# A two-layer graph kernel: the gather table split at row block 10, pauses of three one-column writes, stores by four blocks, the dense branch's flag computed early

## The chip, the core and the metric

The kernel runs on one core of a Trainium2 chip. The metric is device time in microseconds from the first to the last instruction. Before the change it is 416.93 us, the median of three runs (416.52 to 417.89). The profile that is read below is of one further execution, whose instructions span 423.4 us; times of day within it are counted from its first instruction.

## The reference

Two layers over N = 2708 nodes with D = 128 features and an adjacency matrix `adj` that is sparse (each row normalised, a diagonal of self-loops). Layer 0 is hyperbolic: a product of `adj` with node vectors, then functions of norms row by row. Layer 1 passes messages:

```python
XW = mobius_matvec(W, X)
gamma = 2.0 / jnp.maximum(1.0 - jnp.sum(XW * XW, axis=-1, keepdims=True), EPS)
two_mean = (A_hat @ (gamma * XW)) / _clamp_abs(A_hat @ (gamma - 1.0))
...
s = node_feats @ msg_w[:, :D].T
d = node_feats @ msg_w[:, D:].T
messages = jax.nn.gelu(s[:, None, :] + d[None, :, :] + msg_b, approximate=False)
aggregated = jnp.einsum('ijd,ij->id', messages, adj)
combined = jnp.concatenate([node_feats, aggregated], axis=-1)
new_feats = combined @ upd_w.T + upd_b
h = jax.nn.gelu(new_feats, approximate=False) + node_feats
```

Each layer ends with a layer norm of its result plus its input; layer 1 has one more within. A message is needed only where `adj[i, j]` is not zero.

## The kernel before

The nodes are cut into 22 row blocks of 128 (the last has 20 rows). **Layer 0** goes block by block (`layer0`, L327): a load of the block's transposed columns `aT` (L330), its signs (L332), 22 accumulating matmuls with the node vectors (L337), each of two passes. Beside it the kernel finds each block's non-zeros: `keys` (L353) encodes their positions by matmuls of the signs, `extract` (L380) ranks them and lays them into tiles of 128 edges. There are 99 such tiles in all (`TILES`); a tile has a one-hot matrix `R`, and for each of its 128 edges a column index `J` and a flat address `F`.

When a chunk of row blocks is done (`CHUNKS`), `layer0_end` (L471) finishes layer 0 for it, computes `s` and `d` for its rows and stores `d` into `table` in DRAM (L545). It is a generator that is advanced between the halves of the following blocks, by `PARTS`.

**Gathers.** GpSimd reads per tile, with indirect DMAs (`gather`, L195): 128 values of `adj` at the addresses `F` into a column of `V` (L466), and 128 rows of `table` at the indices `J` into `dd` (L675). Behind each gather stands a pause: one addition of two 128x128 tiles into `gap`, which nobody reads (L200). [...]

**Split.** Columns of the first `SPLIT` row blocks are ranked apart from the rest, so that some tiles of each block refer to them alone ("early" tiles; `LATE` counts the others, "late"). A gather of an early tile reads only the first `SPLIT * 128` rows of `table`, so it waits only for the first chunk. Late tiles read the whole table, and wait for all of layer 0.

**Messages.** Tiles are put together by four (a "quad"; `work`, L663): first the early tiles of blocks 0 to 7, then for each block what is left. `fetch` (L670) gathers a quad into one of seven rooms (`RING`). `messages` (L678) handles a quad: matmuls spread `s` to the edges (L687), VectorE makes the weighted one-hot `rv` (L689) and adds the gathered `dd` (L692), ScalarE applies gelu (L693), TensorE sums by row (L702). When a block's last tile is summed, `node` (L619) is queued: the update matmuls into the single bank `sel` (L571 to L574), gelu (L575), layer norms in groups of 8, 6, 4, 2 and 2 blocks (`finish`, L577), and a store of each block (L606). `step` (L633) advances the queue after each quad. An inverse root is computed by 11 VectorE instructions (`rsqrt`, L223), except in the last group, where GpSimd takes a power (`inverse_root`, L561).

**Flag.** The kernel has a dense branch for inputs whose non-zeros don't fit the tiles. From L770 on counts are compared and summed over partitions, and every engine loads the flag (L822) and branches.

A scheduler puts the instructions of each engine into one order, by priority and the order of the code; each engine then runs its own in that order, waiting on semaphores. DMAs that SyncE issues (block loads, table stores, output stores) are in one such order too.

Of the kernel before, what the change touches and what calls it, by code (L numbers as in the profile page):

```python
# [10 lines left out]
F32 = mybir.dt.float32  # L11
# [4 lines left out]
OP = mybir.AluOpType  # L16
AX = mybir.AxisListType

P = 128
# [4 lines left out]
MAGIC = 1597463007.0  # L24
FAR = 6.103033
BREAKS = (11, 18)
CHUNKS = [(0, 13), (13, 18), (18, 22)]
PARTS = (0, 1, 2, 2)
GROUPS = [(0, 8), (8, 6), (14, 4), (18, 2), (20, 2)]
EARLY = 8  # L30
# [2 lines left out]

SPLIT, BITS = 13, 16
RING = 7


def group_of(b):  # L40

    if b == 0:
        return [
            [(0, 1, 8), (1, 2, 8)],
            [(2, 4, 8), (4, 6, 4), (6, 8, 4)],
            [(8, 10, 4), (10, 13, 4), (13, 14, 4), (14, 16, 4)],
            [(16, 19, 4), (19, 22, 4)],
        ]
    if b == 1:
        return [[(0, 4, 4), (4, 8, 2), (8, 13, 2), (13, 22, 2)]]  # L50
    return [[(0, 4, 2 if b < 9 else 1), (4, 13, 1), (13, 22, 1)]]

TILES = [6, 6, 5, 3, 8, 7, 5, 5, 4, 4, 4, 4, 4, 3, 3, 4, 3, 3, 3, 3, 3, 3, 3, 2, 1]
LATE = [0, 0, 2, 3, 3, 3, 2, 2, 2, 2, 2, 2, 2, 1, 1, 2, 1, 1, 2, 2, 2, 2, 2, 1, 1]
SPAN = 8192.0


# [18 lines left out]
def hyperbolic_then_message_kernel(  # L79
# [10 lines left out]
    nc = tc.nc  # L90
# [4 lines left out]
    rows = [min(P, N - b * P) for b in range(NB)]  # L95
# [6 lines left out]
    const = ctx.enter_context(tc.tile_pool(name="const", bufs=1))  # L102
# [7 lines left out]
    w0_sb, wT, rowvec, o = pk[:, :D], pk[:, D : 5 * D].rearrange("p (i d) -> p i d", d=D), {}, 5 * D  # L110
# [13 lines left out]
    ones = const.tile([P, P], F32, name="ones")  # L124
    nc.gpsimd.memset(ones, 1.0)

    nhalf = const.tile([P, 1], F32, name="nhalf")
# [43 lines left out]
    J = const.tile([P, NT], U32, name="J")  # L171
    V = const.tile([P, NT], F32, name="V")
# [17 lines left out]

    of_block = {b: [l for l, v in enumerate(LISTS) if v[0] == b] for b in range(NB)}

    gap = const.tile([P, P], F32, name="gap")

    def gather(o, src, at):  # L195
        last = nc.gpsimd.indirect_dma_start(  # L196
            out=o, out_offset=None, in_=src, in_offset=bass.IndirectOffsetOnAxis(ap=at, axis=0)
        )
        with tc.issue_after(last.ins), tc.high_priority():
            nc.gpsimd.tensor_add(gap, ones, ones)  # L200

    mx = big.tile([P, NB, D], F32, name="mx")
    y = big.tile([P, NB, D + 2], F32, name="y")
# [19 lines left out]
    def rsqrt(v, n, pool=None, two=False):  # L223

        if two:
            h, t, o = (sc.tile([P, 2, NB], F32, name=f"two{k}")[:, :, :n] for k in range(3))
            h = h.bitcast(I32)
        elif pool is None:
            h, t, o = cols(n).bitcast(I32), cols(n), cols(n)
        else:  # L230
            h = pool.tile([P, n], I32, name="rh")
            t = pool.tile([P, n], F32, name="rt")
            o = pool.tile([P, n], F32, name="ro")
        nc.vector.tensor_scalar(h, v.bitcast(I32), 1, None, op0=OP.arith_shift_right)
# [46 lines left out]
    for g, n in quads:  # L281
# [98 lines left out]
    def extract(l):  # L380

        b, groups, c0, wa, wb, t0, n, late = LISTS[l]
# [25 lines left out]
        op = bank("sel", 1)  # L408
# [8 lines left out]
        for k, _ in parts:  # L417
            first = n - late if k and wa else 0
            dl = deg[:, l, k + 1 : k + 2]
            for k0 in range(first, n, 4):  # L420
# [3 lines left out]
                o = flat(R[:, t0 + k0 : t0 + k1, :])  # L424
# [19 lines left out]
        F = small.tile([P, TMAX], U32, name="F", bufs=12)  # L444
        step = 512 // (C + 1)
        for k0 in range(0, n, step):
            k1 = min(n, k0 + step)
            w = k1 - k0
            t = slice(t0 + k0, t0 + k1)
# [13 lines left out]
                F[:, k0:k1], J[:, t], float(b * P * N - 1), rid[:, t], op0=OP.add, op1=OP.add  # L463
            )
        for t in range(t0, t0 + n):
            gather(V[:, t : t + 1], adj.rearrange("i (j o) -> (i j) o", o=1), F[:, t - t0 : t - t0 + 1])  # L466

    x1, x1T, gd = x_sb, xT, nom
    s_nm = mx
# [88 lines left out]
            nc.vector.bn_stats(st[:, k - k0, :], v[:, k, :])  # L558
            nc.vector.bn_aggr(mv[:, k, :], st[:, k - k0, :])

    def inverse_root(ve, n, pool, last):  # L561
        if not last:
            return rsqrt(ve, n, pool)
        o = pool.tile([P, n], F32, name="ro")
        nc.gpsimd.tensor_tensor(o, ve, nhalf[:, 0:1].to_broadcast([P, n]), op=OP.pow)
        return o

    def update(h, k, b, ags):
        up = bank("sel", 1)
        s = slice(b * P, (b + 1) * P)  # L570
# [6 lines left out]
    def finish(h, b0, n, pool, last):  # L577

        mv = mvs.pop(b0)
        ve = pool.tile([P, n], F32, name="ve1")  # L580
        nc.vector.tensor_scalar_add(ve, mv[:, :, 1], LN_EPS)
        rs = inverse_root(ve, n, pool, last)
        yield
        st = pool.tile([P, n, 6], F32, name="st1")
        mw = pool.tile([P, n, 2], F32, name="mv1")
        for k in range(n):
            v = h[:, k, :]
            nc.vector.scalar_tensor_tensor(v, v, mv[:, k, 0:1], rowvec["lw"], op0=OP.subtract, op1=OP.mult)
            nc.vector.scalar_tensor_tensor(v, v, rs[:, k : k + 1], xlb[:, b0 + k, :D], op0=OP.mult, op1=OP.add)
            moments(h, st, mw, [k])  # L590
            if k % 2 and k + 1 < n:
                yield
        ve = pool.tile([P, n], F32, name="ve1")
        nc.vector.tensor_scalar_add(ve, mw[:, :, 1], LN_EPS)
        yield
        rs = inverse_root(ve, n, pool, last)
        if not last:
            nb = pool.tile([P, n], F32, name="nb")
            nc.vector.scalar_tensor_tensor(nb, mw[:, :, 0], -1.0, rs, op0=OP.mult, op1=OP.mult)
        for k in range(n):  # L600
            v, r = h[:, k, :], rows[b0 + k]
            if last:
                nc.vector.tensor_scalar(v, v, mw[:, k, 0:1], rs[:, k : k + 1], op0=OP.subtract, op1=OP.mult)
            else:
                nc.scalar.activation(v, v, AF.Identity, scale=rs[:, k : k + 1], bias=nb[:, k : k + 1])
            nc.sync.dma_start(out[(b0 + k) * P : (b0 + k) * P + r, :], h[:r, k, :])  # L606
        yield

    mvs = {}
# [21 lines left out]
    queue = []  # L631

    def step():  # L633

        for g in list(queue):
            if next(g, queue) is queue:
                queue.remove(g)
# [14 lines left out]
    early, late, soon = {}, {}, set()  # L652
# [10 lines left out]
    work = fours([(b, early[b]) for b in range(EARLY)], True)  # L663
# [3 lines left out]
    done = [0]  # L667
    group = {b: (g0, gn) for g0, gn in GROUPS for b in range(g0, g0 + gn)}

    def fetch():  # L670

        if len(rooms) < (len(work) if whole else ahead):
            dd = edge.tile([P, 4, P], F32, name="dd", bufs=RING)
            for k, (_, t, *_) in enumerate(work[len(rooms)]):
                gather(dd[:, k, :], table[: SPLIT * P] if t in soon else table, J[:, t : t + 1])  # L675
            rooms.append(dd)

    def messages():  # L678

        q, ts = done[0], work[done[0]]  # L680
        done[0] += 1
        w = len(ts)
        dd = rooms[q][:, :w, :]
        X = bank("kx" if q >= ahead and q % 2 else "X").rearrange("p (t d) -> p t d", d=D)[:, :w, :]
        rv = edge.tile([P, 4, P], F32, name="rv", bufs=2)
        for k, (b, t, *_) in enumerate(ts):
            nc.tensor.matmul(X[:, k, :], lhsT=R[:, t, :], rhs=s_nm[:, b, :], start=True, stop=True)  # L687

            nc.vector.tensor_scalar(  # L689
                rv[:, k, :], iotaN, rid[:, t : t + 1], V[:, t : t + 1], op0=OP.is_equal, op1=OP.mult  # L690
            )
        nc.vector.tensor_tensor(dd, X, dd, op=OP.add)  # L692
        nc.scalar.activation(dd, dd, AF.Gelu)  # L693
        for k, (b, t, first, final, before) in enumerate(ts):
            mine = before or b >= EARLY
            if first:
                while len(sums) > 2:
                    step()
                sums[b] = bank("mp", 3)
                if mine:  # L700
                    own(b, sums[b])
            nc.tensor.matmul(  # L702
                sums[b][:, :P], lhsT=dd[:, k, :], rhs=rv[:, k, :], start=(first and not mine), stop=final
            )
            if final and before:
                nc.scalar.copy(gd[:, b, :D], sums.pop(b)[:, :P])  # L706
            elif final:
                g0, gn = group[b]
                queue.append(node(gd[:, g0 : g0 + gn, :D], b - g0, b, g0, gn, [gd[:, b, :D]] if b < EARLY else []))
        fetch()  # L710
        step()

# [48 lines left out]
        fetch()  # L761
    for g, n in quads:
        nc.vector.tensor_add(xlb[:, g : g + n, :D], x1[:, g : g + n, :], wide(rowvec["lb"], n))
    while done[0] < len(work):
        messages()
    while queue:
        step()


    bad = sc.tile([P, NL], F32, name="bad")  # L770
# [18 lines left out]
    for i, v in enumerate(seconds):  # L789
        k = v.shape[1]  # L790
# [27 lines left out]
    nc.vector.tensor_add(tot[:, 0:1], tot[:, 0:1], tot[:, 2:3])  # L818
    flag = sc.tile([P, 1], I32, name="flag")
    nc.vector.tensor_copy(flag, tot[:, 0:1])  # L820

    dense = nc.values_load(flag[0:1, 0:1], min_val=0, max_val=2 * P + 1)  # L822
    with tc.If(dense > 0):
# [100 lines left out]
```

## Time and profile before

| what | value |
|---|---|
| time, median of three | 416.93 us |
| span of the profiled execution | 423.4 us |
| TensorE, VectorE, ScalarE, GpSimd busy | 318.6, 302.9, 200.2, 292.1 us |
| first V gather, first table gather, last gather | 46.7, 199.9, 390.6 us |
| last table store issued | 277.3 us |
| DMA queues' mean rate | 107 GB/s |

The profile has a page and views of the same trace. The page shows the span in 40 slices of 10.6 us, one digit of busy time for each engine. Groups put together the instructions of one line and form: how many, busy time, mean time of one in ns, and the idle time before them with what ended it. A timeline lists instructions in order. A table of stretches gives each engine's busy time within them and the clock that TensorE was granted. [...]

### The profile page before, as it was taken

The page shows a single profiled execution, that of the slowest core. Times are in us where ns is not written, and L with a number is a line of the kernel's source. Part 1 is how long each engine was busy: PE and PEld are TensorE (multiplying, and loading weights), DVE is VectorE, ACT ScalarE, POOL GpSimd, SP SyncE. Part 2 cuts the span into 40 slices and gives each one's busy share as a digit, 9 for nine tenths or more (in the row PEclk, how much of TensorE's full clock was granted, in tenths as well). Part 3 has the DMA queues.
Part 4 walks back from the last instruction along what each step waited for, and adds up shares of the span by engine and source line. Part 5 has one row for each costly group of instructions (what it writes and reads, how often), then busy time and mean ns, then how long its engine had stood idle before and what let it go on. Part 6 is the DMA issues. An engine that isn't in the chain of part 4 may idle for free.

```text
span 423.4 us, 7970 instructions
## 1 busy us (share of the span) xinstructions
PE 318.6 (75%) x2427; PEld 289.3 (68%) x2427; DVE 302.9 (72%) x1524; ACT 200.2 (47%) x538; POOL 292.1 (69%) x495
## 2 busy tenths in 40 slices
PE   3439998999899987799898964292468976969720
PEld 3429887989899977689797854292466866858510
DVE  0996999988667786968989899750426656466890
ACT  1872755766546657369774734150112221222422
POOL 6400588888888880521888888888888988888010
PEclk9957999999989998999899978596575795786655
DMA  8602533445534452615562111011111111112211
GB/s 319 285 1 78 198 137 138 139 137 194 217 121 159 153 217 91 225 52 187 173 234 74 52 38 32 2 44 40 43 43 45 39 43 45 40 43 45 57 38 50
DMA packets 16254, 45.14 MB, mean 107 GB/s; under 512 B 5642, under 2 KB 11166, under 8 KB 13390
## 3 DMA queue, kind: packets, MB, share of 16 engines
q1 hardware_dynamic: 9726, 37.43, 24.3%
q0 software_dynamic: 6336, 6.55, 6.4%
q10 hardware_dynamic: 144, 0.60, 0.4%
q8 instruction: 20, 0.33, 0.3%
q14 instruction: 28, 0.23, 0.2%
HBM read 41.74 MB, written 2.83 MB: 105 GB/s over the span
## 4 chain that ended last, share of the span: by engine, by line
PE 36%; DVE 25%; POOL 12%; ACT 10%; DMA 7%; issue 4%; SPq 2%; DVEq 0%; another core or an unknown queue 0%; POOLq 0%; ACTq 0%
PE mp L337 10%; POOL dd L196 8%; PE kx L364 4%; PE sel L452 4%; PE mp L702 4%; POOL gap L200 4%; DMA aT<-in_adj_t_dram 3%; DMA dd<-table_dram,J 3%; PE X L538 3%; ACT sgn L332 3%; PE X L687 3%; SPq L330 2%; DVE rv L689 2%; DVE R L428 2%; PE kx L285 2%
## 5 line engine op out<-in xcount | busy, mean ns | idle before, releaser
L196 POOL DMA_INDIRECT V<-in_adj_dram,F x99 | 97.8, 988 | 59.6 <-DVE bits L433 29.9
L337 PE MATMUL mp<-y,aT 128*128 128x130 f32 x968 | 131.2, 289 | 2.0 <-DMA aT<-in_adj_t_dram 1.9
L337 PEld LDWEIGHTS mp<-y,aT 128*128 128x128 f32 x968 | 121.3, 200 | 2.3 <-DMA aT<-in_adj_t_dram 2.3
L196 POOL DMA_INDIRECT dd<-table_dram,J x99 | 97.4, 984 | 32.5 <-DMA table_dram<-dt 17.0
L200 POOL TENSOR_TENSOR gap<-ones 128x128 f32<-128x128 f32 x198 | 83.9, 424 | 4.0
L332 ACT ACTIVATE sgn<-aT 128x2816 bf16<-128x2816 f32 x22 | 56.1, 2549 | 3.1 <-DMA aT<-in_adj_t_dram 2.6
L702 PE MATMUL mp<-rv,dd 128*128 128x128 f32 x198 | 37.4, 350 | 20.9 <-ACT dd L693 16.0
L702 PEld LDWEIGHTS mp<-rv,dd 128*128 128x128 f32 x198 | 33.3, 254 | 24.0 <-ACT dd L693 19.4
L693 ACT ACTIVATE dd<-dd 128x512 f32<-128x512 f32 (+1 forms) x25 | 15.5, 624 | 55.5 <-DVE dd L692 48.5
L452 PE MATMUL sel<-z,R 128*128 128x41 f32 (+5 forms) x198 | 30.6, 287 | 13.8 <-DVE R L428 5.0
L364 PEld LDWEIGHTS <-sgn 128*128 128x128 bf16 x484 | 28.7, 100 | 17.2 <-issue 8.9
L689 DVE TENSOR_SCALAR rv<-iotaN,rid,V 128x128 f32<-128x128 f32 x99 | 35.5, 404 | 6.3 <-PE mp L702 6.2
L452 PEld LDWEIGHTS sel<-z,R 128*128 128x128 f32 x198 | 26.4, 197 | 18.4 <-DVE R L428 7.8
L364 PE MATMUL kx<-kd,sgn 128*128 128x128 bf16 x484 | 33.2, 223 | 7.5 <-ACT sgn L332 7.5
L423 ACT ACTIVATE work<-iota,mid 128x256 f32<-128x256 f32 (+3 forms) x54 | 27.6, 560 | 8.3 <-DVE mid L416 6.3
L372 DVE MAX8 top<-kx 128x8 f32<-128x128 f32 (+3 forms) x133 | 25.0, 227 | 8.4 <-PE kx L364 7.1
L692 DVE TENSOR_TENSOR dd<-X,dd 128x512 f32<-128x512 f32 (+1 forms) x17 | 11.5, 679 | 20.1 <-DMA dd<-table_dram,J 17.1
L692 DVE TENSOR_TENSOR dd<-kx,dd 128x512 f32<-128x512 f32 x8 | 5.5, 690 | 27.8 <-DMA dd<-table_dram,J 26.9
L687 PE MATMUL X<-mx,R 128*128 128x128 f32 x134 | 24.4, 322 | 0.0
L687 PEld LDWEIGHTS X<-mx,R 128*128 128x128 f32 x134 | 20.4, 224 | 1.7 <-issue 1.1
L649 PE MATMUL mp<-ident,nom 128*128 128x128 f32 x44 | 10.1, 331 | 12.1 <-ACT nom L706 9.9
L376 ACT ACTIVATE junk_s<-kx 128x384 bf16<-128x384 f32 (+2 forms) x25 | 12.1, 485 | 10.8 <-DVE top L372 6.5
(201 smaller groups left out, 620.2 us busy)
## 6 DMA issues: line engine op xcount, KB each, us to landing
aT<-in_adj_t_dram SPq DMA_DIRECT2D x22, 1408.0 KB
V<-in_adj_dram,F POOLq DMA_INDIRECT x99
dd<-table_dram,J POOLq DMA_INDIRECT x99
xT<-in_x_t_dram SPq DMA_DIRECT2D x2, 704.0 KB
x_sb<-in_x_nm_dram SPq DMA_DIRECT2D x2, 704.0 KB
out_dram<-nom SPq DMA_DIRECT2D x21, 64.0 KB
table_dram<-dt SPq DMA_DIRECT2D x5, 256.0 KB
pk<-in_pack_dram ACTq DMA_DIRECT2D x1, 587.5 KB
```

What stands on the lines that cost most here:

```text
L196: last = nc.gpsimd.indirect_dma_start(out=o, out_offset=None, in_=src, in_offset=bass.IndirectOffsetOnAxis(ap=at, axis=0))
L200: nc.gpsimd.tensor_add(gap, ones, ones)
L332: nc.scalar.activation(sgn, aT, AF.Sign, accum_out=signs[:, b : b + 1])
L337: p = nc.tensor.matmul(op[:, : D + 2], lhsT=aT[:, j, :], rhs=y[:, j, :], start=(j == 0), stop=(j == NB - 1))
L364: nc.tensor.matmul(kp[:, i * P : (i + 1) * P], lhsT=sgn[:, j, :], rhs=kd[:, q, :], start=False, stop=(i == len(groups) - 1 and j == j1 - 1),)
L372: nc.vector.max(top[:, c : c + 8], seg[:, s, :])
L423: nc.scalar.activation(r0, iota[:, k0 * P : k1 * P], AF.Abs, scale=2.0, bias=mid[:, k : k + 1])
L452: nc.tensor.matmul(sp[:, k, :], lhsT=R[:, t0 + k0 + k, :], rhs=z, start=True, stop=True)
L687: nc.tensor.matmul(X[:, k, :], lhsT=R[:, t, :], rhs=s_nm[:, b, :], start=True, stop=True)
L689: nc.vector.tensor_scalar(rv[:, k, :], iotaN, rid[:, t : t + 1], V[:, t : t + 1], op0=OP.is_equal, op1=OP.mult)
L692: nc.vector.tensor_tensor(dd, X, dd, op=OP.add)
L702: nc.tensor.matmul(sums[b][:, :P], lhsT=dd[:, k, :], rhs=rv[:, k, :], start=(first and not mine), stop=final)
```

## The change

Four edits. The split and the end of the first chunk move from row block 13 to 10, with the groups of columns and the counts of late tiles adapted; the second chunk then has 8 blocks instead of 5. This is for the first rows of the table to be ready sooner. The pause after a gather becomes three writes of one column each, into a small tile of its own for each of the two kinds of gather; it is for a shorter pause. Full blocks are stored four at a time. The flag is computed before the last six quads, so that it needn't be at the end, and the last group's inverse roots are computed as the others' are, so that GpSimd has nothing to do there.

```diff
-CHUNKS = [(0, 13), (13, 18), (18, 22)]
+CHUNKS = [(0, 10), (10, 18), (18, 22)]
...
-SPLIT, BITS = 13, 16
+SPLIT, BITS = 10, 16
...
-        return [[(0, 4, 4), (4, 8, 2), (8, 13, 2), (13, 22, 2)]]
-    return [[(0, 4, 2 if b < 9 else 1), (4, 13, 1), (13, 22, 1)]]
+        return [[(0, 4, 4), (4, 10, 2), (10, 16, 2), (16, 22, 2)]]
+    return [[(0, 4, 2 if b < 9 else 1), (4, 10, 1), (10, 22, 1)]]
...
-LATE = [0, 0, 2, 3, 3, 3, 2, 2, 2, 2, 2, 2, 2, 1, 1, 2, 1, 1, 2, 2, 2, 2, 2, 1, 1]
+LATE = [0, 0, 4, 3, 3, 3, 2, 2, 2, 2, 2, 2, 2, 1, 2, 2, 2, 2, 2, 2, 2, 2, 2, 1, 1]
...
-    gap = const.tile([P, P], F32, name="gap")
+    gap = [const.tile([P, 3], F32, name=f"gap{k}") for k in range(2)]
...
         with tc.issue_after(last.ins), tc.high_priority():
-            nc.gpsimd.tensor_add(gap, ones, ones)
+            for k in range(3):
+                nc.gpsimd.memset(gap[kind][:, k : k + 1], 0.0)
...
-        rs = inverse_root(ve, n, pool, last)
+        rs = rsqrt(ve, n, pool)
...
-            nc.sync.dma_start(out[(b0 + k) * P : (b0 + k) * P + r, :], h[:r, k, :])
+            if r < P:
+                nc.sync.dma_start(out[(b0 + k) * P : (b0 + k) * P + r, :], h[:r, k, :])
+            elif k % 4 == 3 or k + 1 == n or rows[b0 + k + 1] < P:
+                k0 = k - k % 4
+                to = out[(b0 + k0) * P : (b0 + k + 1) * P, :]
+                nc.sync.dma_start(to.rearrange("(k p) d -> p k d", p=P), h[:, k0 : k + 1, :])
...
-    while done[0] < len(work):
+    while done[0] < len(work) - 6:
         messages()
-    while queue:
-        step()
...
     nc.vector.tensor_copy(flag, tot[:, 0:1])
+
+    while done[0] < len(work):
+        messages()
+    while queue:
+        step()
```

More of the change, by code (lines that the diff above doesn't have):

```diff
@@ L191, in hyperbolic_then_message_kernel, with gather @@
     of_block = {b: [l for l, v in enumerate(LISTS) if v[0] == b] for b in range(NB)}
-    gap = const.tile([P, P], F32, name="gap")
-    def gather(o, src, at):
+    gap = [const.tile([P, 3], F32, name=f"gap{k}") for k in range(2)]
+    def gather(o, src, at, kind):
         last = nc.gpsimd.indirect_dma_start(
@@ L465, in extract @@
         for t in range(t0, t0 + n):
-            gather(V[:, t : t + 1], adj.rearrange("i (j o) -> (i j) o", o=1), F[:, t - t0 : t - t0 + 1])
+            gather(V[:, t : t + 1], adj.rearrange("i (j o) -> (i j) o", o=1), F[:, t - t0 : t - t0 + 1], 0)
     x1, x1T, gd = x_sb, xT, nom
@@ L559, in moments @@
             nc.vector.bn_aggr(mv[:, k, :], st[:, k - k0, :])
[L561 to L566, printed above, removed]
     def update(h, k, b, ags):
@@ L595, in finish @@
         yield
-        rs = inverse_root(ve, n, pool, last)
+        rs = rsqrt(ve, n, pool)
         if not last:
@@ L674, in fetch @@
             for k, (_, t, *_) in enumerate(work[len(rooms)]):
-                gather(dd[:, k, :], table[: SPLIT * P] if t in soon else table, J[:, t : t + 1])
+                gather(dd[:, k, :], table[: SPLIT * P] if t in soon else table, J[:, t : t + 1], 1)
             rooms.append(dd)
```

## The prediction

> **What bounds the kernel now.** I read the 40 slices first, then the groups, the GpSimd queue in order of time, and the sums of stretches.
>
> ```profile
> PE   3439998999899987799898964292468976969720
> DVE  0996999988667786968989899750426656466890
> POOL 6400588888888880521888888888888988888010
> PEclk9957999999989998999899978596575795786655
> ```
>
> Up to slice 23 (243 us) TensorE and VectorE are full: 22 row blocks of layer 0. From then to slice 37 neither is, but GpSimd (POOL) stays at 8 without a break from slice 19 on. The 8 is a queue that never waits: its gaps are the steps between its own instructions.
>
> ```profile
> L196 POOL DMA_INDIRECT V<-in_adj_dram,F x99 | 97.8, 988 | 59.6 <-DVE bits L433 29.9
> L196 POOL DMA_INDIRECT dd<-table_dram,J x99 | 97.4, 984 | 32.5 <-DMA table_dram<-dt 17.0
> L200 POOL TENSOR_TENSOR gap<-ones 128x128 f32<-128x128 f32 x198 | 83.9, 424 | 4.0
> ```
>
> 198 gathers of 0.97 us (median), each followed by a 0.41 us pause. The queue in order of time, lines from three places:
>
> ```profile
> 14.49 0.10 POOL L188 MEMSET cap<- 128x1 f32 x1
> 14.52 0.10 POOL L189 MEMSET least<- 128x1 f32 x1
> ...
> 180.68 0.96 POOL L196 DMA_INDIRECT V<-in_adj_dram,F  x1 [0.30 <-issue]
> 181.94 1.05 POOL L196 DMA_INDIRECT V<-in_adj_dram,F  x1 [0.30 <-issue]
> 199.95 0.95 POOL L196 DMA_INDIRECT dd<-table_dram,J  x1 [16.96 <-DMA table_dram<-dt]
> ...
> 343.15 0.42 POOL L200 TENSOR_TENSOR gap<-ones 128x128 f32<-128x128 f32 x1
> 343.73 0.97 POOL L196 DMA_INDIRECT dd<-table_dram,J  x1 [0.16 <-issue]
> 344.71 0.41 POOL L200 TENSOR_TENSOR gap<-ones 128x128 f32<-128x128 f32 x1
> ```
>
> Columns: start, duration, engine and line, idle time before. Gather, pause and 0.16 us of issue make the pitch; the last 71 gathers start from 280.65 to 390.57, 1.570 us apart. At 180.68 and 181.94 two gathers happen to stand without a pause: 1.26 us apart. At 199.95 GpSimd has waited 17 us for the table of the first 13 blocks; after that it never catches up. The last table store is issued by 277.7:
>
> ```profile
> 233.19 44.52 SPq L545 DMA_DIRECT2D table_dram<-dt  x3
> 391.44 26.22 SPq L606 DMA_DIRECT2D out_dram<-nom  x22
> ```
>
> so the whole table is there at about 280, but the first of the 63 gathers that need it goes out only at 293.1, behind 8 early ones and 9 of V. From 293.1 to the last gather's end at 391.6 the others wait on gathers, with TensorE 75% busy at a mean clock of 0.69:
>
> ```profile
> 293.00:391.00 98.00, 73.08 (x388) 65.11 (x388) 52.46 (x201) 19.79 (x57) 86.98 (x125) 0.69 0.17 43
> 391.60:423.40 31.80, 10.07 (x40) 7.88 (x39) 19.91 (x145) 9.88 (x29) 1.92 (x4) 0.55 0.17 48
> ```
>
> (stretch, us, busy time of PE, PEld, DVE, ACT, POOL, clock, DMA). Then comes a tail of 31.8 us. The time is: start of the late gathers, plus number times pitch, plus tail.
>
> **What the Trainium skill says.** "SBUF — State Buffer", section "Who interferes with whom": VectorE and GpSimd share one port pair as an exclusive lock; a VectorE instruction with two SBUF inputs contends with a GpSimd one that reads SBUF, not with one that only writes. The trace agrees: L689 takes 419 ns (median) where it overlaps a pause, 335 over a gather alone, 310 with GpSimd idle. Over all pauses the excess against the same forms elsewhere is 19 us of VectorE time. "Perfetto Trace Analysis", section "DMA Instruction — SWDGE (GPSIMD)": a gather's row ends when its descriptors are written, not when data has landed. The trace agrees: the last gather ends at 391.62, its reader starts at 394.06, 2.4 us later. "TensorE: Matmul & The Clock Gate", Part 1: the array is throttled until activity releases it. Here only partly: from 324.0 to 333.6 TensorE is busy throughout at 0.50, then at 1.00.
>
> **The change part by part.**
>
> *Pauses.* 198 additions (412 ns) become 594 one-column writes. L188 and L189 give the price: 95 ns long, 33 ns apart, so three take 95 + 2 x 33 = 161 ns. Pitch: 967 + 20 + 161 + 160 = 1.31 us. Lower bound: the two gathers without a pause, 1.26. Upper bound: three writes that don't overlap, 967 + 3 x 95 + 160 = 1.41. I take 1.31, because writes without inputs queued behind one another overlap in this trace. The columns differ, and the tiles for V and dd differ, so a write waits only for a write one gather ago.
>
> *Split at 10.* Early tiles go from 36 to 34, late ones from 63 to 65, quads from 25 to 26. In the built order the table stores of the first chunk stand behind 15 block loads on SyncE's queue, not 18; loads are about 8.5 us apart, so the first table gather moves from 200 to about 170. Behind these stores wait the loads of blocks 15 and 16, as now the load of block 18 (192.8) waits behind stores at 183.6 to 190.2; TensorE waits for it, a shift in time but no more of it. From there 62 gathers (34 early, 28 of V) at 1.31 take 81 us: GpSimd is through by about 257, the last V indices being ready at 252.5 (L462), and waits for the whole table. The layer's second end now has 8 blocks, not 5; same work in all, and VectorE's order from the last block to the last store is nearly the one of before (16 rv, 4 dd), so the whole table stays at 280. The additions no longer block VectorE there: 1.4 us in each 20 us from 40 to 240, some of it on the path; I take 2. Late gathers start at 278 instead of 293: -15. Either edit alone would do nearly this (57 gathers from 200 at 1.31 end at 275; 62 from 170 at 1.57 at 267), so it is counted once.
>
> *The late stage.* 64 x 1.31 + 0.97 = 84.8 us against 98.5: -13.7. Last gather ends at 362.8.
>
> *No GpSimd at the end.* Two powers (0.79 and 0.70 us, about 1.0 each with their semaphores) become 11 VectorE instructions each. The same chain standing alone at the layer's end (269.08 to 271.85) takes 2.8 us; the second does here too, +1.8; the first runs between a neighbour group's, +0.9. Behind them: the last normalisation and the last stores. +2.7.
>
> *Flag early.* Out of the tail go two matmul pairs and a copy between 403.8 and 405.0, and four VectorE instructions of 0.15: -1. SyncE's load of the flag (0.50) and its assertion (0.4) move ahead of all stores; they wait there for a flag that is made six quads before the end, and the first store (391.4 now) comes later than that. GpSimd's closing drain, 7.64 us from 414.92 to 422.56 and now the last thing to end, begins right after the last pause and is hidden.
>
> *Stores.* 22 become 8; at the end four, not eight, of about 0.45 us each. Now from the last normalisation (415.77) to the end it is 7.6 us; then two issues (0.9), landing (about 2), SyncE's closing (1.0) and the barrier (0.8): 4.7. With the flag, -2.9. A group of four waits for its fourth block; only the last group, of 1 block and 20 rows, is on the path.
>
> *Last quad.* It has one tile instead of three: add, gelu and matmuls shorter by about 1.5.
>
> Tail: 31.8 + 2.7 - 1 - 2.9 - 1.5 = 29.1. End: 362.8 + 29.1 = 391.9 against 423.4, -31.5. On the measured 416.9 that is **385 us**.
>
> **Rivals.**
> - *TensorE becomes the bound.* For: it was busy 73.1 of 98 us; 65 of 63 tiles make 75.4, which is 89% of 84.8, and it stayed 9.6 us at half clock while full. Against: seven rooms of four tiles (7 x 5.2 us) absorb a lag, and at full clock it is much quicker: 71 matmuls from 333.6 to 343.0 at 1.00, 39 from 324.0 to 333.6 at 0.50. If the clock stays, about 9 us come back, or the same with a pitch of 1.41 (64 x 0.10 = 6.4): 393.
> - *Layer 0 also gets faster.* For: 1.4 us of every 20 of VectorE, and no bunch of 13 blocks at 160 to 200, where block loads fell to 10.5 us apart. Some 10 us earlier table: 375.
> - *The gain is only the pitch or only the start.* If the whole table comes later because the second end has 8 blocks in the last four, by some 10 us: 395.
> - *The short pause starves someone.* With the queue denser, gathers or VectorE could block one another: the slowest gather now takes 1.24 us. At 1.24 + 0.16 + 0.16 + 0.2 for waits, 1.76 x 64 + 1 + 278 + 29 + 5 of stalls on VectorE = 426 in the profile, 419 measured: slower. Against: around 180.68, without a pause, gathers took 0.96 and 1.05 and L527 ran at 0.28 us each.
>
> **How the numbers follow.** Forecast (380 to 390): 0.48. TensorE or the longer pause (390 to 397): 0.22. Faster layer 0 (370 to 380): 0.15. Late table (393 to 400): 0.08. Starved: 0.05; no net change: 0.02. The range 373 to 398 leaves out the starved and unchanged cases and the outer parts of two others, under 0.2. Faster 0.93, same 0.02, slower 0.05.
>
> **What would show it.** Gathers 1.31 apart in the late stage; an idle time of GpSimd before the first late gather, ended by the table store (10 to 25 us); that gather at 275 to 281; no GpSimd after the last pause but the drain; L689 near 335 ns; a tail of 29. Wrong if the late stage shows GpSimd waiting for rooms (PE L702), if a write costs more than 0.1 us, or if the last table store moves past 285.

## The result, and the profile after

The changed kernel takes **372.4 us** (median, 370.8 to 374.7), the kernel before beside it 417.4: a ratio of 0.892, interval 0.885 to 0.898. It was forecast faster, and it is, but by 45 us where 32 were forecast; it lies just below the range. The sums that the forecast had for the late stage and for the end came out within some 2 us. What it missed is layer 0, to which it gave 2 us of gain.

The 40 slices of the kernel after, now 9.2 us each:

```profile
PE   2618998999999999999998897409858997996700
DVE  0998898978768796877787878983725586477994
POOL 7500087988898717078889878940888888888000
PEclk9955999999999999999999998957985699599755
```

TensorE (PE) is at 9 almost without a break up to slice 23 (221 us), and a hole in GpSimd (POOL) at slices 26 and 27 (240 to 258 us, counting slices from 0) now parts layer 0 from the late stage. Before there was none: GpSimd was behind from 200 us on. The groups (busy time in us, mean ns of one; then idle time before them):

```profile
L197 POOL DMA_INDIRECT V<-in_adj_dram,F x99 | 95.8, 968 | 69.1 <-DVE F L464 44.8
L197 POOL DMA_INDIRECT dd<-table_dram,J x99 | 96.2, 971 | 27.4 <-PE X L687 13.4
L202 POOL MEMSET gap<- 128x1 f32 x594 | 36.3, 123 | 0.1
L689 DVE TENSOR_SCALAR rv<-iotaN,rid,V 128x128 f32<-128x128 f32 x99 | 30.9, 359 | 4.0 <-PE mp L702 4.0
```

The pauses cost GpSimd 36 us instead of 84. The 13.4 us are the hole. The view puts it down to a matmul, but the first late gather starts 3.2 us after the last table store is issued (254.44), and so it does, by 3.1 to 3.3 us, in every run below in which GpSimd is waiting by then, with that store anywhere from 254 to 350 us; so I read it as a wait for the table. GpSimd in order of time at that place:

```profile
257.64 0.94 POOL L197 DMA_INDIRECT dd<-table_dram,J  x1 [13.25 <-PE X L687]
258.58 0.26 POOL L202 MEMSET gap<- 128x1 f32 x3
258.90 0.95 POOL L197 DMA_INDIRECT dd<-table_dram,J  x1
259.85 0.17 POOL L202 MEMSET gap<- 128x1 f32 x3
```

And two stretches, the late stage and the tail (us, busy time of PE, PEld, DVE, ACT and POOL, clock, DMA share, GB/s):

```profile
257.60:340.30 82.70, 70.87 (x451) 64.11 (x450) 51.92 (x220) 24.77 (x74) 73.13 (x258) 0.83 0.21 52
340.30:369.10 28.80, 7.14 (x34) 5.79 (x34) 23.18 (x162) 9.20 (x26) 0.26 (x3) 0.61 0.18 53
```

65 gathers, 1.276 us apart, and then 28.8 us. In the prediction and here, the late gathers are all those from the first whole-table one on, 63 before and 65 after. The prediction says that all 63 need the whole table; by `LATE` only 43 of them do (48 after), and the others are early tiles of blocks 8 to 21 that stand behind the first in the queue. The count that the late stage is priced by holds all the same. Where the time went, from the two profiles (the profiled execution before took 425.2 us, 8 us more than the median, and the new profile of it in e9 shows where some of that lay):

| profile, us | before | e9, before again | after | forecast |
|---|---|---|---|---|
| last table store issued | 277.3 | 273.5 | 254.4 | table there at 278 |
| first gather of the whole table | 293.1 | 290.1 | 257.6 | 278 |
| late stage, gathers in it | 98.5, 63 | 98.8, 63 | 82.7, 65 | 84.8, 65 |
| tail after the last gather | 31.8 | 32.4 | 28.8 | 29.1 |
| span | 423.4 | 421.2 | 369.1 | 391.9 |

### The profile page after: what moved, and what is told of

Same layout as the page of the kernel before. It is cut to its first block, busy times and chain, and to the rows that moved or that the text cites. A ratio compares the mean times of both kernels' runs of the same rounds, so it can differ in the third digit from the quotient of the medians.

```text
span 369.1 us, 8354 instructions
## 1 busy us (share of the span) xinstructions
PE 295.7 (80%) x2427; PEld 272.9 (74%) x2427; DVE 276.9 (75%) x1544; ACT 199.5 (54%) x537; POOL 239.0 (65%) x889
## 4 chain that ended last, share of the span: by engine, by line
PE 52%; DVE 13%; DMA 11%; POOL 11%; ACT 9%; issue 3%; POOLq 0%; DVEq 0%; ACTq 0%; SPq 0%
PE mp L339 22%; POOL dd L197 9%; DMA aT<-in_adj_t_dram 8%; PE kx L366 6%; PE sel L454 5%; PE mp L702 4%; ACT sgn L334 3%; PE X L540 3%; PE X L687 3%; DMA dd<-table_dram,J 2%; PE kx L287 2%; POOL gap L202 2%; ACT junk L294 2%; DMA xT<-in_x_t_dram 1%; PE kx L360 1%
## 5 line engine op out<-in xcount | busy, mean ns | idle before, releaser
L339 PE MATMUL mp<-y,aT 128*128 128x130 f32 x968 | 126.8, 283 | 1.6 <-DMA aT<-in_adj_t_dram 1.6
L339 PEld LDWEIGHTS mp<-y,aT 128*128 128x128 f32 x968 | 117.3, 194 | 2.0 <-DMA aT<-in_adj_t_dram 2.0
L197 POOL DMA_INDIRECT dd<-table_dram,J x99 | 96.2, 971 | 27.4 <-PE X L687 13.4
L702 PE MATMUL mp<-rv,dd 128*128 128x128 f32 x198 | 33.2, 320 | 14.0 <-ACT dd L693 12.3
L702 PEld LDWEIGHTS mp<-rv,dd 128*128 128x128 f32 x198 | 29.4, 226 | 15.9 <-ACT dd L693 13.9
L202 POOL MEMSET gap<- 128x1 f32 x594 | 36.3, 123 | 0.1
L689 DVE TENSOR_SCALAR rv<-iotaN,rid,V 128x128 f32<-128x128 f32 x99 | 30.9, 359 | 4.0 <-PE mp L702 4.0
L693 ACT ACTIVATE dd<-dd 128x512 f32<-128x512 f32 (+2 forms) x26 | 15.7, 607 | 30.6 <-DVE dd L692 30.6
L454 PEld LDWEIGHTS sel<-z,R 128*128 128x128 f32 x198 | 25.8, 192 | 6.1 <-DVE R L430 3.7
L687 PE MATMUL X<-mx,R 128*128 128x128 f32 x132 | 22.3, 305 | 0.5 <-DVE dd L692 0.5
L457 DVE TENSOR_TENSOR work<-sel,place 128x120 f32<-128x120 f32 (+11 forms) x29 | 11.2, 387 | 9.6 <-PE sel L454 9.1
L622 ACT COPY agT<-mp 128x128 f32<-128x128 f32 x22 | 5.8, 262 | 18.6 <-PE mp L702 15.5
```

The source lines that it names most:

```text
L197: last = nc.gpsimd.indirect_dma_start(out=o, out_offset=None, in_=src, in_offset=bass.IndirectOffsetOnAxis(ap=at, axis=0))
L202: nc.gpsimd.memset(gap[kind][:, k : k + 1], 0.0)
L339: p = nc.tensor.matmul(op[:, : D + 2], lhsT=aT[:, j, :], rhs=y[:, j, :], start=(j == 0), stop=(j == NB - 1))
L454: nc.tensor.matmul(sp[:, k, :], lhsT=R[:, t0 + k0 + k, :], rhs=z, start=True, stop=True)
L689: nc.vector.tensor_scalar(rv[:, k, :], iotaN, rid[:, t : t + 1], V[:, t : t + 1], op0=OP.is_equal, op1=OP.mult)
L702: nc.tensor.matmul(sums[b][:, :P], lhsT=dd[:, k, :], rhs=rv[:, k, :], start=(first and not mine), stop=final)
```

## First batch: the parts one by one, and a disturbance

The kernel before unchanged (e1), with the new pauses alone (e2), with the split alone (e3), and the kernel after with the old addition as its pause (e4). The edits (in these cuts, lines that only declare `gap` or pass on the kind of gather are left out):

```diff
 e2: the kernel before, with
-            nc.gpsimd.tensor_add(gap, ones, ones)
+            for k in range(3):
+                nc.gpsimd.memset(gap[kind][:, k : k + 1], 0.0)
 e3: the kernel before, with CHUNKS, SPLIT, the groups and LATE of the kernel after
 e4: the kernel after, with
-            for k in range(3):
-                nc.gpsimd.memset(gap[kind][:, k : k + 1], 0.0)
+            nc.gpsimd.tensor_add(gap, ones, ones)
```

> The kernel before, profiled once more. The recorded profile spans 423.4 us while its timed runs lie at 416.5 to 420.3, so some of the 23 us by which the last table store moved (277.3 to 254.4) may belong to that one execution. If it does (theory C), this profile spans about 416 and its last table store stands at about 268 to 272. If not, 423 and 277 again. Time 417 in any case.

> The kernel before with the pauses as three one-column writes and nothing else. Theory A (the addition's reads hold the port pair that VectorE shares, and that slowed layer 0): last table store 10 to 15 us earlier than in the kernel before, VectorE's L689 near 340 ns, late gathers 1.27 apart, time about 386 to 390. Theory B (layer 0 gained from the spread of its end over chunks of 10, 8 and 4 blocks): last table store within 3 us of the kernel before, time about 395 to 398 (14 us from the late gathers' start, 15 from their pitch, less the waiting behind). Table gathers start near 195 in both.

> The kernel before with the split at block 10 (chunks, groups of columns, late counts) and nothing else. Theory A: last table store within 4 us of the kernel before, late gathers at 1.57 from right behind it, 65 of them take 102 us, time about 405 to 409. Theory B: last table store 10 to 15 us earlier, time about 393 to 397.

> The changed kernel with one 128x128 addition as its pause again, the rest as changed. Theory A: the last table store goes back by 10 to 15 us from 254.4, to about 266, and the late stage takes 102 instead of 83 us: about 402 to 406. Theory B: the store stays at about 256, only the late stage grows: about 391 to 394.

Beside a kernel before of 425.1 us in this batch: e1 425.1; e2 **506.2** (1.192, interval 1.185 to 1.198); e3 437.9 (1.029, 1.022 to 1.035); e4 443.0 (1.045, 1.037 to 1.053). By these, the pauses alone and the split alone each make the kernel slower, and all the edits together make it 11% faster. That was too odd to build on, above all e2: its instructions stand in the same order as before's on TensorE, VectorE and ScalarE. TensorE in e2 in order of time (start, duration; in brackets the idle time before and what ended it):

```profile
124.40 0.90 PE L365 MATMUL kx<-kd,sgn 128*128 128x128 bf16 x13
126.04 0.22 PE L365 MATMUL kx<-kd,sgn 128*128 128x128 bf16 x1 [0.74 <-issue]
126.75 0.22 PE L365 MATMUL kx<-kd,sgn 128*128 128x128 bf16 x1 [0.49 <-issue]
127.46 0.28 PE L365 MATMUL kx<-kd,sgn 128*128 128x128 bf16 x2 [0.50 <-issue]
```

Thirteen matmuls in 0.9 us, then one or two at a time at steps of 0.71 or 1.4 us, until 131.8. They wait for no semaphore ("issue"), and meanwhile VectorE and ScalarE wait for TensorE. Such stretches are found at 93 to 98, 126 to 131 and 278 to 288 us, and elsewhere results of TensorE reach their reader 4 to 10 us late; in the profiles of before and after there is no such stretch in layer 0. So either e2's program does this to itself, or the batch was disturbed. None of the times that were expected of e1 to e4 came out; e1's profile repeats the first one of this kernel (span 424.4 us, last table store at 278.9). The same programs had to be run again.

## Second batch: after, pauses alone, no pause, a long write

```diff
 e5: the kernel after, unchanged; e6: e2 again
 e7: the kernel after, with
-        with tc.issue_after(last.ins), tc.high_priority():
-            for k in range(3):
-                nc.gpsimd.memset(gap[kind][:, k : k + 1], 0.0)
 e8: the kernel after, with
+    gap = const.tile([P, 346], BF16, name="gap")
-            for k in range(3):
-                nc.gpsimd.memset(gap[kind][:, k : k + 1], 0.0)
+            nc.gpsimd.memset(gap, 0.0)
```

> The changed kernel with nothing edited, beside the kernel before on the same chip. In e2 to e4 TensorE crawled now and then (one matmul each 0.71 us, results 4 to 10 us late), and never in the profile of the changed kernel. Theory P (the crawl belongs to a program, its order of instructions together with its pauses): 372 us, 0.89 of the kernel before, no crawl, last table store at 254. Theory C (the crawl belongs to the chip that batch of runs had, which the changed kernel didn't meet): where the pause-only kernel crawls again, this one crawls too, with its last table store past 290 and 1.0 of before or more.

> The kernel before with three one-column writes as the pause, a second time. Its instructions stand in the order of the kernel before on TensorE, VectorE and ScalarE, all of them. Theory P: 1.19 of the kernel before again, last table store near 350. Theory C: on a chip without the crawl 386 to 398, 0.92 to 0.95; on one with it 1.19 again and the changed kernel slow as well.

> The changed kernel without any pause between gathers; all else in the same order on every engine. Theory P1 (pauses only cost GpSimd time): the pitch of the late gathers falls from 1.276 to 1.25 as in the stretches of e4 where gathers stand without a pause, 65 x 0.026 = 1.7 us, so 370 to 372. Theory P2 (pauses keep TensorE from crawling; shorter ones brought the crawl in e2): with none it crawls, 1.1 of before or more, 460 us.

> The changed kernel with one write of a 128x346 BF16 tile as the pause: as long as the old addition (about 0.42 us) but reading nothing. Layer 0's order is that of the changed kernel. Theory L (length of the pause sets layer 0's pace): as e4, last table store near 300, 1.04 of before. Theory R (the addition's reads slow VectorE, its length doesn't matter): last table store near 254 as in the changed kernel, late gathers at 1.57 again, 65 x 0.3 = 19 us more: 390 to 393, 0.93 of before.

The kernel before took 417.4 us here. e5: 372.6, 0.893 (0.888 to 0.897). e6: **374.8**, 0.898 (0.895 to 0.901): the program that took 506 in the first batch. It is also 11 us below the 386 to 398 that were expected without the crawl: the pauses alone bring nearly all of the gain. So the crawl is no property of that program. Nor is it bound to one chip as far as the records tell: they give the first batch and the two later ones the same chip number, and the later ones don't have it. I leave e1 to e4 out of the accounts below; what caused the crawl stays open.

e7: 371.6, 0.889 (0.885 to 0.892). Without any pause the late gathers are 1.255 us apart, with three writes 1.276. Theory P1 holds and P2 falls: in these runs the pauses bring nothing, and the new ones cost 0.02 us each.

e8: 395.1, 0.947 (0.944 to 0.950). Late gathers are 1.534 apart, so the late stage takes 99.1 instead of 82.7 us (+16.4), but the last table store is at 260.4, 3.3 us behind e5. The start is nearer to theory R's 254 than to theory L's 300, the time 2 us over R's range. So a pause as long as the addition, but which only writes, costs layer 0 little here; the old order (e15 below) shows more. The pauses' groups in e8 and in e10, the addition in the next batch, show that their lengths are alike:

```profile
L201 POOL MEMSET gap<- 128x346 bf16 x198 | 81.9, 414 | 0.9
```

```profile
L201 POOL TENSOR_TENSOR gap<-ones 128x128 f32<-128x128 f32 x198 | 85.7, 433 | 4.8
```

## Third batch: the same questions without the disturbance

```diff
 e9: the kernel before, unchanged; e10: e4 again; e11: e3 again
 e12: the kernel after, with
+            if kind == 0:
+                nc.gpsimd.tensor_add(gapv, ones, ones)
+            else:
+                for k in range(3):
+                    nc.gpsimd.memset(gap[kind][:, k : k + 1], 0.0)
```

> The kernel before, unchanged, for a profile on a chip where it takes 417 us. Both profiles of it so far are of 425 us executions. Theory C2 (those two carry some of the crawl): span near 416, last table store near 270 instead of 277, late TensorE results fewer. Theory N (profiling alone costs the 8 us): span 424, last table store 277 to 279 again.

> e4 once more (the changed kernel with the 128x128 addition as the pause), for a chip without the crawl. Order of layer 0 as in the changed kernel and in e8. Theory R (the addition's two reads slow VectorE and so layer 0; a write of the same length does not): last table store 274 to 278, late gathers 1.57 apart, 372.6 + 18 + 19 + 1 = 409 to 412, 0.98 of before. Theory L (only GpSimd's time counts): as e8, last table store 260 to 262, 65 x 0.04 = 2.6 us over e8: 397 to 399, 0.953 of before.

> e3 once more (the kernel before with the table split at block 10, the chunks and the counts of late tiles), for a chip without the crawl. By what the pauses alone gave (374.8 us against 372.6 for all edits) the split and the end are worth 2 us together. Theory A (the parts add): e10 plus 2 to 5 us for the end, no better than 1.5% from the kernel before: 411 to 416 under R, 400 to 404 under L.

> The changed kernel with the addition as the pause behind layer 0's gathers of V only; the rows' gathers keep the three writes. Order as in the changed kernel on TensorE, VectorE and ScalarE. Theory R: last table store 270 to 278, late gathers 1.28 apart, 388 to 392, 0.935 of before. Theory L: last table store 257 to 260, 373 to 376, 0.897 of before.

e9: 422.4 by two runs, while the same program beside it has a median of 417.6 in seven (ratio 1.011, 1.001 to 1.021). Here two copies of one kernel differ by 1%, one of them run only twice (the copies in the first batch, 18 and 23 runs, agreed within 0.2%); I take 1% as the limit below which kernels are not told apart. Its profile has the last table store at 273.5 and spans 421.2 us, between the two theories, so of the first profile's 277.3 some 4 us were its own. In the same way e5 has this store at 257.1 and the first profile of the same kernel at 254.4: times within one profile are good to 3 or 4 us.

e10: **407.4**, 0.975 (0.967 to 0.983). e11: **407.4**, 0.974 (0.966 to 0.982). e12: 383.3, 0.911 (0.902 to 0.920), with the last table store at 268.6, 11.5 us behind e5, and the late stage unchanged at 82.8. In e10 the table is 3 us and the time 2 us ahead of theory R's ranges, in e12 1 and 5 us; both are far from L's. e11 is 4 us faster than it was expected to be under R: the split alone is worth 10 us, where the expectation had split and end together at 2. The stretch from the first gathers to the last table store (columns as above), for the kernel before and for the pauses alone, whose instructions stand in the same order:

```profile
46.00:273.50 227.50, 197.48 (x1749) 182.06 (x1748) 192.43 (x1004) 140.89 (x355) 177.50 (x249) 0.93 0.40 135
```

```profile
46.00:254.10 208.10, 189.08 (x1745) 176.15 (x1743) 166.59 (x997) 139.24 (x355) 151.76 (x525) 0.95 0.43 149
```

VectorE (the third of the pairs) does the same thousand instructions in 166.6 us instead of 192.4. The stretch gets 19.4 us shorter. What TensorE waits for in this stretch, in e9 and then in e6, leaving out the one long wait behind the last block (us in total, times, longest):

```profile
PE sel L452 <- DVE R L428: 7.0, 8, 2.6
PE mp L337 <- DMA aT<-in_adj_t_dram: 3.3, 2, 1.8
PE sel L452 <- DVE R L426: 2.4, 1, 2.4
```

```profile
PE mp L338 <- DMA aT<-in_adj_t_dram: 2.5, 2, 2.1
PE sel L453 <- DVE R L429: 1.8, 4, 0.9
PE sel L453 <- DVE R L427: 1.7, 1, 1.7
```

TensorE sat waiting for VectorE's one-hot matrix `R` for 9.4 us, and does for 3.5 with short pauses. In all its idle time in the stretch falls from 30.0 to 19.0 us (stretch less busy time) and its busy time by 8.4, the same number of matmuls; why these take less is not resolved, their ends being modelled. The granted clock is 0.93 and 0.95 in the two lines; if the busy time went with it, that would be some 4 of the 8.4 us (an estimate, 0.02 of 197.5), and whether the clock is cause or result no run shows. The same wait, with layer 0 in the changed kernel's order, in e10 (addition), e8 (long write), e14 (copy, from the next batch) and e5 (short writes):

```profile
PE sel L453 <- DVE R L429: 8.7, 8, 3.6
```

```profile
PE sel L453 <- DVE R L429: 5.1, 7, 1.8
```

```profile
PE sel L453 <- DVE R L429: 3.7, 4, 2.1
```

```profile
PE sel L454 <- DVE R L430: 2.4, 2, 1.5
```

It falls in the same order as the time of the last table store: 271.0, 260.4, 258.2 and 257.1 us. By the load of the last block 14.1 of the 19.4 us have been won (214.2 against 200.1 us).

## Fourth batch: which property of the addition, and what the split is worth

```diff
 e13: the kernel after, with
-                nc.gpsimd.memset(gap[kind][:, k : k + 1], 0.0)
+                nc.gpsimd.tensor_add(gap[kind][:, k : k + 1], ones[:, k : k + 1], ones[:, k : k + 1])
 e14: e10, with
-            nc.gpsimd.tensor_add(gap, ones, ones)
+            nc.gpsimd.tensor_copy(gap, ones)
 e15: the kernel before, with
-    gap = const.tile([P, P], F32, name="gap")
+    gap = const.tile([P, 346], BF16, name="gap")
-            nc.gpsimd.tensor_add(gap, ones, ones)
+            nc.gpsimd.memset(gap, 0.0)
 e16: the kernel after, with CHUNKS, SPLIT, the groups and LATE of the kernel before
```

> The changed kernel with three one-column additions in place of the three one-column writes; the order on every engine is the same. Theory R1 (what slows VectorE is the time for which GpSimd reads and writes its tile: a one-column addition takes little longer than a one-column write): last table store 256 to 260, 372 to 376, 0.895 of before. Theory R2 (each reading instruction costs VectorE, whatever its length, and there are three for one): last table store past 270, 388 or more.

> The changed kernel with a copy of the 128x128 tile as the pause: one operand read where the addition reads two. Order as in e10 on every engine. Theory R (number of reads): layer 0 between e8 and e10, last table store 262 to 268. Theory F (the addition's arithmetic, not its reads): as e8, 260. Both: late gathers between 1.4 and 1.57 apart, 385 to 402.

> The kernel before with one write of a 128x346 BF16 tile as the pause; layer 0 in the order of the kernel before. If e8 against e10 holds here too: last table store 256 to 259 instead of 273.5, late gathers still 1.53 apart: 417.6 - 15 - 2 = 400, 0.958 of before. If e8's fast layer 0 came of the split: last table store 270 or later, 413 to 416.

> The changed kernel with the table split back at block 13 and the old chunks and late tiles: pauses and end without the split. Theory S0 (with short pauses GpSimd waits for the table either way, the split brings nothing): 374.8 - 4 (the pause-only kernel's tail of 33.4 falls to 29) = 370 to 372, as the changed kernel. Theory S1 (the split brings some us): 374 to 378, 0.5 to 1.5% over the changed kernel.

e13: **414.5**, 0.989 (0.982 to 0.995); e14: 388.9, 0.927 (0.922 to 0.933); e15: 408.3, 0.974 (0.968 to 0.980); e16: 373.2, 0.889 (0.883 to 0.894), beside a kernel before of 419.6.

e13 meets R1's number for the table and misses its time by 38 us; it is the most instructive of the misses. VectorE is left in peace (170.7 us) and the last table store comes at 259.9, as R1 said. But a one-column addition on GpSimd is dear. Its group, and the queue in the late stage:

```profile
L202 POOL TENSOR_TENSOR gap<-ones 128x1 f32<-128x1 f32 x594 | 109.1, 219 | 3.7
```

```profile
300.35 0.47 POOL L202 TENSOR_TENSOR gap<-ones 128x1 f32<-128x1 f32 x3
300.98 0.96 POOL L197 DMA_INDIRECT dd<-table_dram,J  x1 [0.15 <-issue]
301.97 0.47 POOL L202 TENSOR_TENSOR gap<-ones 128x1 f32<-128x1 f32 x3
302.59 0.96 POOL L197 DMA_INDIRECT dd<-table_dram,J  x1 [0.15 <-issue]
```

Three take 0.47 us together where three writes take 0.17, so late gathers are 1.655 us apart; GpSimd is behind again (the first one starts at 274.7, 14.8 us after the table was stored) and the late stage takes 106.9 us. So R1 has layer 0 right and the price of its instruction wrong.

e14, one operand read instead of two, has VectorE at 177.8 and the table at 258.2, no later than e5 within what the runs tell apart. So the table is where theory F (the arithmetic and not the reads) had it, 4 us ahead of R's range: that any read of a whole tile costs layer 0 its time is not shown. The copy is also shorter, 0.29 us to 0.41, and no run parts a second operand from the arithmetic and from this length. e15 confirms e8 in the old order (262.3, where the addition gives 273.5), but with short writes the table is there at 254.1 to 255.8 in this order, so the long write costs 6.5 to 8 us, not 3. Its time was forecast at 400: GpSimd, with its gathers 1.53 us apart, has not caught up by then, and the first whole-table gather starts only at 276.3. e16 is theory S0's, 1 us over its range. All runs of the last three batches, by what the pause is:

| pause | run | VectorE busy, 46 us to last table store | last table store | first whole-table gather | pitch | us |
|---|---|---|---|---|---|---|
| two-operand addition, both tables | e9 (before) | 192.4 | 273.5 | 290.1 | 1.577 | 417.4 to 422.4 |
| | e11 (split alone) | 192.9 | 271.0 | 275.4 | 1.563 | 407.4 |
| | e10 (split and end) | 193.3 | 271.0 | 275.4 | 1.566 | 407.4 |
| the same behind V only | e12 | 188.5 | 268.6 | 271.8 | 1.278 | 383.3 |
| long write | e15 (old split) | 173.7 | 262.3 | 276.3 | 1.528 | 408.3 |
| | e8 | 175.5 | 260.4 | 263.6 | 1.534 | 395.1 |
| copy | e14 | 177.8 | 258.2 | 261.5 | 1.473 | 388.9 |
| short additions | e13 | 170.7 | 259.9 | 274.7 | 1.655 | 414.5 |
| short writes | e6 (old split, old end) | 166.6 | 254.1 | 258.9 | 1.289 | 374.8 |
| | e16 (old split) | 167.7 | 255.8 | 260.6 | 1.275 | 373.2 |
| | e5 (after) | 167.4 | 257.1 | 260.3 | 1.278 | 372.6 |
| none | e7 | 167.1 | 258.0 | 261.0 | 1.255 | 371.6 |

By and large, the more the pause takes from VectorE, the later the table is: some 26 us taken and 14 to 19 us later for the addition, 7 to 10 taken and 1 to 8 later for the copy and the long write, and no difference between short writes and none that stands out of the 1% by which copies of a kernel differ. The order of copy, long write and short additions is not told apart. The chip is not what makes the difference: e5 to e8 ran on one chip by the records and e9 to e16 on another, where e16 repeats e6's and e5's times, and the kernel before took 417.4, 417.6 and 419.6 us in the three batches. The trade that the pause makes with VectorE is not the one with GpSimd: e8 and e10 hold up GpSimd for the same 0.41 us and differ by 10.6 us in the table, and e13 holds GpSimd up longest and takes less from VectorE than any of the long pauses.

The split is worth 10 us alone (e11), and nothing once pauses are short: e16 and e5 are equal. In that equality two parts cancel: with the split the late stage has two gathers more and is 2.7 us longer (80.0 to 82.7), and the tail behind its shorter last quad is 3.0 us shorter (31.5 to 28.5). What the split is worth alone comes from the queue: with additions it lets GpSimd be nearly through before the table is there (4.4 us from store to first whole-table gather, not 16.6); short pauses do that too (4.8 in e6). The end is worth too little to show in the time (e10 and e11 are equal, e6 and e16 differ by 0.4% in us and 1% as ratios), though the tails of these pairs differ by 0.6 and 1.9 us.

## Why the prediction missed, step by step

**The table at 280 less 2: this is the step that failed.** "The additions no longer block VectorE there: 1.4 us in each 20 us from 40 to 240, some of it on the path; I take 2." The prediction names the contention (the Trainium skill, "SBUF — State Buffer", section "Who interferes with whom"), measures its excess as 19 us of VectorE time, and then puts 2 of it on the path; it gives no reason for the 2. TensorE was nearly full in layer 0, but with waits for VectorE's `R` in it. Measured: VectorE 25.8 us less and the table 19.4 us earlier by the pauses alone (e9 to e6), 13.9 in the new order (e10 to e5), of which the addition behind V makes 11.5 (e12). The rival "layer 0 also gets faster" had the mechanism and named the very 1.4 us in 20; its size of 10 us was between a half and three quarters of what there was. In the profile after, the first late gather is 20.4 us ahead of the forecast; the stage adds 2.1 and the tail 0.3, together the 22.8 us between 391.9 and 369.1. Not all of this is the step's: the profile before is of an execution 8.3 us longer than the median and the one after of one 1.6 us shorter. By medians the miss is 13 us (385.4 to 372.4), and a table that comes 14 to 19 us earlier by the pauses instead of 2 makes up 12 to 17, the whole of it within what the profiles scatter.

One reading beside it is wrong too, with no effect on the number. L689, given as the sign that the trace agrees with that section, is not plainly its case of two SBUF inputs: it has one 128x128 input and two of one column, and a pause that only writes lengthens it more than the addition does (last section).

**The start, apart from that: right.** GpSimd was to catch up and wait for the table, with an idle time of 10 to 25 us; it is 13.3. It waits from 244 us on, where the prediction had it through by 257. "Either edit alone would do nearly this" held as well: e11 and e6 each remove 12 us of lag, and e5 doesn't add them. What wasn't foreseen is that for this reason the split is worth nothing in the whole.

**The second end of 8 blocks: right.** It delays nothing that shows: with equal pauses the table is 2.5 us earlier (e9 to e11) or 1.3 later (e16 to e5), neither more than profiles of one kernel differ by.

**The pitch: right, 1.276 for 1.31.** A set of three writes takes 0.17 us, the 161 ns that were worked out; the gathers are 0.94 to 0.95 us where they stand in a row, 0.03 less than the group's mean. The lower bound of 1.26, two gathers without a pause, is what e7 shows for all (1.255). A write has some 0.11 us (median of the group in e16) where it was priced at 0.095. "If a write costs more than 0.1 us" was one of the signs of being wrong; it came true without harm, because the three overlap.

**The tail: right in sum, 28.8 for 29.1; in part by luck.** The split, with its last quad of one tile, takes 2.6 us from it (e9 to e11, 32.4 to 29.8) or 3.0 (e16 to e5), where 1.5 were forecast. Powers, flag and stores together take 0.6 (e11 to e10) or 1.9 (e6 to e16), where 1.2 were; no run parts these three.

**The rivals that didn't come.** TensorE as bound: it is busy 70.9 of 82.7 us at a clock of 0.83, and GpSimd's waits for rooms in the late stage (PE L702) come to 0.6 us, four of at most 0.2. A starved queue: e7 has the densest one and loses nothing.

**How the miss fell outside.** The faster layer 0 was given 15% and 370 to 380 us, and the range ended at 373, so it cut off a part of a case that was held to be possible.

## What to carry to other kernels

An instruction put in to pass time on one engine should be judged by what it takes from the others: count the engine that shares its operands' path over the whole stage, not the engine that it runs on. When an excess on a second engine has been measured over a stage in which that engine is 85% busy and feeds the bound, keep all of it in the range, not a tenth. And test parts against the unchanged kernel's own time in the same batch, again when a part alone gives the opposite of the whole.

## What the runs showed of the hardware

- The long write without an operand slows one kind of VectorE instruction more than the addition does. The group of `rv` in e10, e8 and e14:

```profile
L688 DVE TENSOR_SCALAR rv<-iotaN,rid,V 128x128 f32<-128x128 f32 x99 | 36.4, 415 | 5.2 <-PE mp L701 5.2
```

```profile
L688 DVE TENSOR_SCALAR rv<-iotaN,rid,V 128x128 f32<-128x128 f32 x99 | 37.6, 478 | 3.8 <-PE mp L701 3.0
```

```profile
L688 DVE TENSOR_SCALAR rv<-iotaN,rid,V 128x128 f32<-128x128 f32 x99 | 31.5, 359 | 4.8 <-PE mp L701 4.7
```

  415 ns with additions, 478 with long BF16 writes, 359 with copies, 360 in e5 with short writes. The same page of the Trainium skill says that an instruction with two SBUF inputs contends with one that reads, not with one that only writes, and that `tensor_scalar` can take the whole shared pair. Added up from the traces by operation, from 46 us to the last table store, the first agrees in the main: SCALAR_TENSOR_TENSOR and TENSOR_TENSOR, which have two tensor inputs (a few of them in PSUM), take 57.6 and 41.6 us in e5, 69.8 and 47.4 with additions (e10), but 61.1 and 43.8 with long writes (e8); MAX8, with one, takes 23.0 to 23.5 in all three. The second fits e8, where TENSOR_SCALAR takes 60.7 us, to 47.0 in e5 and 54.2 in e10; that it takes the pair here is not shown. In e8 these longer instructions lie partly beside others, so that VectorE's busy time as a whole grows by only 8. e14 reads as many bytes per operand as e10 and costs `rv` nothing, and the two kinds above 5.4 and 2.3 us, less than half of the addition's 12.2 and 5.8; by this page's rules alone I can't tell why a copy is so much gentler than an addition. That stays open.
- On GpSimd a one-column addition takes 0.22 us on the mean and three in a row 0.47 (e13); a one-column write 0.12 and three 0.17 (after).
- TensorE can fall into a crawl of single matmuls 0.7 or 1.4 us apart that lasts 5 to 10 us (e2), with nothing in its way that the profile shows. The program in whose trace it stands took 506 us then and 375 in a later run; no later trace has it.
- GpSimd's closing drain took 8.0 us in the kernel after (340.2 to 348.2) and hides behind the last layer norms; before, it was among the last things to end (414.9 to 422.6 of 423.4).
